# Attention block and selective scan on one core: side steps spaced by their TensorE work, matmuls in smaller pieces

## The chip, the cores and the metric

The kernel runs on one core of a Trainium2 chip. The metric is device time in microseconds: the median over repeated executions. The engines are TensorE (PE in the profile), VectorE (DVE), ScalarE (ACT), GpSimd (POOL) and SyncE (SP), which here issues every DMA. Each engine works off its own instructions in order; between engines, semaphores make one wait for the other.

## The reference

Sixteen images x of 256 channels by 32 x 32 positions go through two layers, each behind a group norm and with a residual (the norms have 16 groups and no weights). In short:

```
# layer 0, per image: tokens n = 1024, channels c = 256
tok  = groupnorm(x).T + pos_embedding
q, k, v = split(layernorm(tok) @ w_qkv)            # 4 heads of 32
out  = softmax(q @ k.T / sqrt(32)) @ v
tok  = out @ w_out + b_out + tok
tok  = gelu(layernorm(tok) @ w_ff1 + b_ff1) @ w_ff2 + b_ff2 + tok
x    = x + tok.T
# layer 1, per image: L = 1024 positions, 512 inner channels, 64 states
xs   = groupnorm(x).T + (rel_h + rel_w)
ctx  = sigmoid(conv1d(xs, gate_w, width 3) + gate_b)
u, z = split(xs @ in_proj_w.T)
u    = silu(depthwise_conv(u, width 4) + conv_b)
dt, Bm, Cm = split(u @ x_proj_w.T, [16, 80])
delta = softplus(dt @ dt_proj_w.T + dt_proj_b);  A = -exp(A_log)
for each position t:                               # for 512 channels d, 64 states n
    h[d, n] = exp(delta[d] * A[d, n]) * h[d, n] + delta[d] * u[d] * Bm[n]
    y[d]    = sum over n of h[d, n] * Cm[n]
x    = x + ((y + u * D) * silu(z)) @ out_proj_w.T * ctx
```

## The kernel before

The scan is the backbone. For one image the recurrence has 512 x 64 = 32768 rows of 1024 positions. The kernel puts two channels with their 64 states on the 128 partitions and cuts time in two halves of 512 positions. A *unit* is four channels over one half: two DVE scans of 128 x 512. There are 256 units per image and 4096 in all; the loop `for n, (b, t, k, q, i) in enumerate(units)` writes them out one after the other. Eight units with the same q are a *block*. I call the 256 units of one image a *pass*. What surrounds unit n in program order is:

- `load(n + 6)`: SP issues the DMA that spreads delta times u over the partitions (`dub`, 512 KB, seven buffers).
- `inputs(n + 4)`: POOL multiplies `dub` by B.
- `scan(n, 0)` and `scan(n, 1)`: the two DVE scans, which read the decay `a` from PSUM and `dub`, and write `h`.
- `decay(n + 2)`: two matmuls (L880) spread delta, and two ACT Exps (L883) make the decay in place. The four PSUM buffers `a` come free as the scans of unit n have read them.
- A piece of *side work*, see below.
- A piece of `outputs`: the products of the states with C for the block before (L927), with a copy to SBUF (L935), a second set of matmuls that turn the result (L939), another copy (L947) and the stores.

The side work is everything else: while image b is being scanned, the rest of image b - 1 (the multiplication with silu(z), the output projection, the gate and the store: `gate_and_store`) and all that comes before the scan for image b + 1 (`first_norm`, `attention_layer`, `scan_inputs`). These are Python generators, and each `yield` ends a step and gives a number, the share of the step just written out. Before the change the loop keeps an account: each unit adds `rate` (the sum of all shares divided by 247 units, 1.11 for most images), and steps are written out as long as the account is above zero:

```
due += rate
while due > 0.0:
    due -= next(side, 1e9)
```

So two steps can fall into one unit, and a long share can be followed by a step in the very next unit. The order of instructions on PE, ACT, DVE and POOL is then fixed as written: a manual dependency chains each instruction to the one before it on its engine. SP's queue keeps its order as well. PSUM is shared: four banks for `a`, one for `yb` (products with C), one for attention's values, and two (`mm`) for all of the side work.

The names that matter below: L387 takes the row maxima of the scores (written by L406), L474 and L482 are the transposed scores and their Exp, L462 the values (together "st/av"); L282 and L306 are the two vector parts of a layer norm, L267 the end of a group norm, L263/L264 and L299/L301 the Ln and Exp between; L506 is the reciprocal of the softmax denominators, which pass through DRAM; L599 multiplies z by its sigmoid (matmul L610, tanh L615); L645 are the convolution taps on u (matmul L631), L685 its silu; L660 the gate's convolution as matmuls; L697 the projection of u to dt, B and C; L716 to L759 the softplus of delta, its split into three bf16 pieces `pc` and the product `du`. `gate_and_store` begins with L790 (add u times D) and L794 (times z), each on 128 x 1024 for four parts d, their operands ys, us, zs fetched by DMA, and ends with the projection L819 and its use in L806/L808. `spread_c` (L909) writes C into the sparse weights `cd` by eight ACT copies, twice per image. `outputs` before the change hands out a block in six pieces:

```
for half in range(2):
    # s = 0, 1: 32 matmuls; yield; s = 2, 3: 32 matmuls
    # copy y2 <- yb; yield
    # 16 turning matmuls; yield (after half 0)
# copy yo <- yb, three more yields, then the stores
```

Of the kernel before, what the change touches and what calls it, by code (L numbers as in the profile page):

```python
# [52 lines left out]
def attention_then_scan_kernel(  # L53
# [176 lines left out]
    def group_norm(src, dst):  # L230
        def sum_of(part, s, k):
            view = part.rearrange("p (h g t) -> p g h t", g=NG, t=2)
            nc.vector.tensor_reduce(s[:, k, :], view, AX.XY, ALU.add)

        def mean_of(s, name):
            m = psum(f"{name}_ps")[:, :NG]
            for k in range(KC):
                nc.tensor.matmul(m, avg, s[:, k, :], start=(k == 0), stop=(k == KC - 1))
            return m

        per = C / (C * L / NG)
        s = small.tile([P, KC, NG], F32, name="gn_s", tag="gn_s")
        sum_of(src[0], s, 0)
        yield 1.2
        sum_of(src[1], s, 1)
        m = mean_of(s, "gn_m")
        yield 1.2
        s = small.tile([P, KC, NG], F32, name="gn_q", tag="gn_s")
        qs = []
        nc.vector.tensor_scalar(m, m, per, None, ALU.mult)  # L250
        for k in range(KC):
            nc.vector.tensor_tensor(grouped(dst[k]), grouped(src[k]), over_group(m), ALU.subtract)
            q = work("gn_sq")
            nc.scalar.activation(q, dst[k], AF.Square)
            qs.append(q)
            yield 1.2
        sum_of(qs[0], s, 0)
        yield 1.2
        sum_of(qs[1], s, 1)
        del qs, q  # L260
        v = mean_of(s, "gn_v")
        yield 1.2
        nc.scalar.activation(v, v, AF.Ln, bias=eps, scale=per)  # L263
        nc.scalar.activation(v, v, AF.Exp, scale=-0.5)  # L264
        yield 1.5
        for k in range(KC):
            nc.vector.tensor_tensor(grouped(dst[k]), grouped(dst[k]), over_group(v), ALU.mult)  # L267
            yield 1.2


    def layer_norm(src, dst, g, b):
        def mean_of(parts, name):
            m = psum(name)
            for k in range(KC):
                nc.tensor.matmul(m, avg, parts[k], start=(k == 0), stop=(k == KC - 1))
            return m

        def centre(h, m):
            qs = []
            for k in range(KC):  # L280
                d = dst[k][:, hs(h)]
                nc.vector.tensor_tensor(d, src[k][:, hs(h)], m, ALU.subtract)  # L282
                q = hwork("ln_sq")
                nc.scalar.activation(q, d, AF.Square)
                qs.append(q)
            return qs

        m = mean_of([t[:, hs(0)] for t in src], "ln_m")
        yield 1
        q0 = centre(0, m)  # L290
        m = mean_of([t[:, hs(1)] for t in src], "ln_m")
        yield 1.2
        q1 = centre(1, m)
        vs = [mean_of(q0, "ln_v")]
        yield 1.2
        vs.append(mean_of(q1, "ln_v"))
        yield 1
        for v in vs:
            nc.scalar.activation(v, v, AF.Ln, bias=eps)  # L299
        for v in vs:  # L300
            nc.scalar.activation(v, v, AF.Exp, scale=-0.5)  # L301
        yield 2
        for h in range(2):
            for k in range(KC):
                d = dst[k][:, hs(h)]
                nc.vector.tensor_tensor(d, d, vs[h], ALU.mult)  # L306
                nc.scalar.activation(d, d, AF.Identity, bias=col(b, k), scale=col(g, k))
            yield 1.2
# [12 lines left out]
    def first_norm(b):  # L321
        xs, tok = [], []
        kept = state[b]["kept"] = dram.tile([C, L], F32, name="kept", tag="kept")
        if "x" in state[b]:
            xs = state[b].pop("x")
        else:
            for go in fetches(xs, x[b]):
                go()
            yield 0.7
        gn = [work("gn") for _ in range(KC)]  # L330
        yield from along(group_norm(xs, gn), fetches(tok, pos))
        for k in range(KC):
            nc.vector.tensor_tensor(tok[k], tok[k], gn[k], ALU.add)
            nc.sync.dma_start(kept[ts(k, P), :], tok[k])
            yield 1.4

    def attention_layer(b):
# [32 lines left out]
        for i, (t, scale) in enumerate(((q4, DH**-0.5), (k4, 1.0))):  # L370
            for hf in range(2):
                ps = psum("qk_ps")
                for k in range(KC):
                    nc.tensor.matmul(
                        ps, wqk_s[:, k, ts(i, P)], xn[k][:, hs(hf)], start=(k == 0), stop=(k == KC - 1)
                    )
                nc.scalar.activation(t[:, hs(hf)], ps, AF.Copy, scale=scale)
                yield 1
# [19 lines left out]
        for c in range(2 * NJ):  # L398
            for hf in range(2):
                maxima()  # L400
                for g in range(2):
                    waiting.append((psum("s_ps"), g, c, hf))
                for h in range(HEADS):
                    g, e = divmod(h, 2)
                    r = ts(h, DH)
                    nc.tensor.matmul(  # L406
                        waiting[g][0][ts(e, 64)], q4[r, ts(c, 64)], k4[r, hs(hf)],
                        start=True, stop=True,
                    )
                if to_space:  # L410
                    to_space.pop(0)()
                yield 1.1
# [6 lines left out]
        yield 1.2  # L419
# [6 lines left out]
        yield 0.7  # L426
# [3 lines left out]
        for g in range(2):  # L430
# [11 lines left out]
            yield 1  # L442
# [10 lines left out]
        for pair in range(HEADS // 2):  # L453
# [3 lines left out]
            for hf in range(2):  # L457
# [11 lines left out]
                for j in range(NJ):  # L469
# [16 lines left out]
                    yield 1.5  # L486
# [11 lines left out]
        yield 0.6  # L498
        nc.sync.dma_start(few, rows[0])
        yield 0.6  # L500
        tok = []
        for go in fetches(tok, kept):
            go()
            yield 0.8
        yield 0.8
        nc.vector.reciprocal(few, few)  # L506
        yield 0.6
        nc.sync.dma_start(rows[1], few)
        yield 0.6
        for h in range(HEADS):  # L510
            nc.sync.dma_start(sums[ts(h, DH)], den[1, h : h + 1].partition_broadcast(DH))
            if h % 2 == 1:
                yield 0.8
        yield 0.8
        yield 0.8
        outs = []
        for hf in range(2):
# [11 lines left out]
            yield 1.5  # L529
# [11 lines left out]
        for hf in range(2):  # L541
            nc.vector.tensor_tensor(xs[hf], xs[hf], tok[hf], ALU.add)
            ps = psum("f1_ps")
            for k in range(KC):
                nc.tensor.matmul(
                    ps, wff1_s[:, k, :], xn[k][:, hs(hf)], start=(k == 0), stop=(k == KC - 1)
                )
            f1.append(ps)
            yield 1.5
# [17 lines left out]
    def scan_inputs(b):  # L567
# [18 lines left out]
        for k in range(KC):  # L586
            nc.vector.tensor_tensor(body[k], body[k], rels[k], ALU.add)
            yield 1.4
# [15 lines left out]
        for d in range(ND):  # L604
            z = work("z")
            for hf in range(2):
# [10 lines left out]
                yield 1  # L617
# [33 lines left out]
        def gate(o, hf, q):  # L651
            if (hf, q) == (0, 0):
                gates["g"] = work("g")
            if q == 0:
# [3 lines left out]
            for i in range(3 * KC):  # L658
                k, t = divmod(i, 3)
                nc.tensor.matmul(  # L660
                    ps[:, ts(q, C)], xp[k][:, ds(first + t, P, 4)], wg_s[:, k, t, :],
                    start=(i == 0), stop=False,
                )
            nc.tensor.matmul(ps[:, ts(q, C)], one_row, gate_b, start=False, stop=True)
# [10 lines left out]
        for d in range(ND):  # L675
            for t in range(2):
# [3 lines left out]
                yield 1.6  # L680
            tap(d, 2)
            nc.scalar.activation(ups[d][:, :L], us[d], AF.Tanh)
            gate(d // 2, d % 2, 0)
            yield 1.6
# [3 lines left out]
            gate(d // 2, d % 2, 1)  # L688
            yield 1.6
# [3 lines left out]
        for hf in range(2):  # L693
            for dst, lo, n in ((dt, 0, RANK), (bc, RANK, 2 * NS)):
                ps = psum("x_ps", n)
                for d in range(ND):
# [3 lines left out]
                    )  # L700
                nc.scalar.copy(dst[:n, hs(hf)], ps)
                yield 1.6
# [31 lines left out]
        for d in range(ND):  # L734
            items = [more(d, *items[0]), begin(d, 1)]
            yield 1
            items[1] = more(d, *items[1])
            rest(*items[0])
            yield 1.4
# [3 lines left out]
            yield 1.7  # L743
# [4 lines left out]
            yield 1.4  # L748
# [4 lines left out]
            yield 1.4  # L753
# [3 lines left out]
            yield 1.4  # L757
# [8 lines left out]
            yield 1.4  # L766
# [4 lines left out]
    GATE = 26.6  # L771

    def gate_and_store(b):
# [8 lines left out]
        for go in come[:4]:  # L782
            go()
            yield 0.7
# [3 lines left out]
        for d in range(ND):  # L788
# [3 lines left out]
            yield 1.3  # L792
# [3 lines left out]
            yield 1.3  # L796
            if d + 1 < ND:
                come.pop(0)()
                yield 0.7
# [13 lines left out]
        for o in range(KC):  # L813
            for hf in range(2):
                ps = psum("m_ps")
                for q in range(2):
# [10 lines left out]
                    yield 1.1  # L827
# [89 lines left out]
    def outputs(b, t, k, q):  # L917
        cd, hbuf = now["cd"], now["h", q % 2]
        out4 = yb[:, 256:].rearrange("p (j a m e) -> p a e j m", a=2, j=2, e=4)
        if t == 0:  # L920
            nc.scalar.copy(now["last"][:, ds(64 * k + 16 * q, 16)], hbuf[:, :, TB - 1])
        for half in range(2):
            for s in range(4):
# [8 lines left out]
                if s == 1:  # L932
                    yield
            y2 = blk.tile([P, 256], F32, name="y2", tag="y2")
            nc.scalar.copy(y2, yb[:, :256])  # L935
            yield
            for e in range(4):
                for s in range(4):
                    nc.tensor.matmul(  # L939
                        out4[32 * s : 32 * s + 16, half, e],  # L940
                        y2[:, 64 * s + e : 64 * s + 64 : 4], turn[:, e],
                        start=True, stop=True,
                    )
            if half == 0:
                yield
# [16 lines left out]
    steps = sum(prepare(0))  # L962
# [9 lines left out]
    side, rate, due = iter(()), 0.0, 0.0  # L972
    for n, (b, t, k, q, i) in enumerate(units):
        at = n % UNITS
        if at == 0:
            parts = [prepare(b + 1)] if b + 1 < B else []
            total = steps * len(parts)
            if b > 0:
# [3 lines left out]
                total += GATE  # L982
            side = chain(*parts)
            rate, due = total / (UNITS - AHEAD - 3), 0.0
# [14 lines left out]
        if at >= (1 if b + 1 < B else 8):  # L999
            due += rate  # L1000
            while due > 0.0:
                due -= next(side, 1e9)
# [85 lines left out]
```

## Time and profile before

| | |
|---|---|
| median of three runs | 13563.83 us (13536.5 to 13569.5) |
| profiled execution | 13520.45 us, its span 13518.5 us |
| DVE busy | 12165.9 us, 90% of the span |
| PE busy (weight loads) | 10686.8 us, 79% (5389.6 us, 40%) |
| POOL busy | 9761.5 us, 72% |
| ACT busy | 7916.0 us, 59% |
| DMA | 209 GB/s in the mean, queue 1 at 60.5% of its 16 engines |
| two scans of a unit | 1199 ns each in the first half of time, 1260 in the second |

The first unit begins 377 us into the span and the last ends at 13472 us, so that nearly the whole time is the unit loop. A busy share over such a loop is a mean over stages that have different limits, and the stages repeat with every image. It is therefore of more use to cut one image's 256 units into their stages, and to ask in each of them what the DVE, the fullest engine, waits for. "Granted clock" is the share of TensorE's full clock that the record shows as granted. A wait is put down to the releaser that came last by the profile; where the engine named had long been done, it was another.

### The profile page before, as it was taken

To read this page: it belongs to the slowest core of one execution; us is meant where nothing else is said; L and a number is where in the kernel's file an instruction comes from. 1 tells how busy PE (TensorE), PEld (TensorE's weight loads), DVE (VectorE), ACT (ScalarE), POOL (GpSimd) and SP (SyncE) were. 2 spreads that over 40 slices of the span, in tenths; PEclk is the share of its full clock that TensorE was granted. 3 is DMA by queue.
4 is the path that set the end of the run, shared out by engine and by line. 5 is a ranking of instruction groups with operands and counts; after the bars stand their busy time and mean duration, and the time that the engine had idled before them with its cause. 6 is when DMAs were issued, how large, how long until landed. Compare 5 with 4: busy or idle time off the path is not lost. (4 is left out here: it accounts for less than half of the span.)

```text
span 13518.5 us, 429250 instructions
## 1 busy us (share of the span) xinstructions
PE 10686.8 (79%) x186800; PEld 5389.6 (40%) x186800; DVE 12165.9 (90%) x11652; ACT 7916.0 (59%) x13941; POOL 9761.5 (72%) x4118
## 2 busy tenths in 40 slices
PE   7787878878787787877878778787787878878767
PEld 3343344433444334443344433434444344433434
DVE  3899999899998999999999898999999999989998
ACT  3666665656655565555656556566465665656654
POOL 0777767777777777767777677776777767777697
PEclk8786877868788686876868778687786877868777
DMA  1566566565665666656666566655666566665666
GB/s 64 202 205 234 197 212 218 203 227 203 208 217 200 228 205 213 212 201 223 208 223 205 198 222 206 235 199 199 220 207 234 193 205 220 206 231 198 209 233 224
DMA packets 1001896, 2820.85 MB, mean 209 GB/s; under 512 B 175810, under 2 KB 319427, under 8 KB 1000004
## 3 DMA queue, kind: packets, MB, share of 16 engines
q1 hardware_dynamic: 1000004, 2793.39, 60.5%
q8 instruction: 1460, 23.92, 0.7%
q14 instruction: 432, 3.54, 0.1%
HBM read 2514.18 MB, written 261.62 MB: 205 GB/s over the span
## 5 line engine op out<-in xcount | busy, mean ns | idle before, releaser
L871 POOL TENSOR_TENSOR dub<-dub,bt 128x1024 f32<-128x1024 f32 x4096 | 9706.4, 2386 | 3702.5 <-DMA dub<-dus 3218.5
L883 ACT ACTIVATE a<-a,acol 128x512 f32<-128x512 f32 x8192 | 5063.6, 659 | 3830.4 <-PE a L880 3800.3
L893 DVE TENSOR_TENSOR_SCAN h<-a,last,dub 128x512 f32<-128x512 f32 x4096 | 4927.0, 1260 | 129.1 <-issue 88.0
L893 DVE TENSOR_TENSOR_SCAN h<-a,dub 128x512 f32<-128x512 f32 x4096 | 4691.0, 1199 | 281.1 <-issue 160.7
L880 PE MATMUL a<-pieces,pick 48*128 48x512 bf16 x8192 | 2983.3, 468 | 2447.9 <-DVE h L893 2371.4
L927 PEld LDWEIGHTS yb<-h,cd 128*32 128x32 f32 x131072 | 2568.5, 136 | 1945.6 <-issue 1700.1
L927 PE MATMUL yb<-h,cd 128*32 128x64 f32 x131072 | 2967.1, 259 | 28.8 <-issue 19.7
L880 PEld LDWEIGHTS <-pick 48*128 48x128 bf16 x8192 | 521.6, 96 | 2607.9 <-issue 2396.6
L406 PE MATMUL s_ps<-k,q 32*64 32x512 f32 x4096 | 890.4, 719 | 59.2 <-DVE mx L387 58.3
L939 PEld LDWEIGHTS yb<-turn,y 128*16 128x16 f32 x32768 | 408.7, 119 | 993.6 <-ACT y L935 493.2
L935 ACT COPY y<-yb 128x256 f32<-128x256 f32 x1024 | 383.3, 374 | 718.3 <-PE yb L927 714.3
L387 DVE TENSOR_REDUCE mx<-s_ps 128x1 f32<-128x512 f32 x1024 | 643.4, 669 | 24.4 <-PE s_ps L406 22.2
L939 PE MATMUL yb<-turn,y 128*16 128x32 f32 x32768 | 538.2, 212 | 103.2 <-ACT y L935 99.4
L474 PE MATMUL st_ps<-sp 33*128 33x512 f32 x2048 | 598.0, 627 | 14.1 <-ACT pt L482 13.9
L462 PE MATMUL av<-pt,vv 128*64 128x512 f32 x2048 | 577.3, 642 | 5.5 <-ACT sums L451 3.3
L482 ACT ACTIVATE pt<-st_ps 128x512 f32<-128x512 f32 x1024 | 556.7, 604 | 40.0 <-PE st_ps L474 38.8
L660 PE MATMUL g_ps<-w,xp 128*128 128x256 f32 x1536 | 447.4, 447 | 0.0
L406 PEld LDWEIGHTS s_ps<-k,q 32*64 32x64 f32 x4096 | 206.8, 148 | 580.1 <-DVE mx L387 540.3
L660 PEld LDWEIGHTS g_ps<-w,xp 128*128 128x128 f32 x1536 | 389.5, 328 | 100.5 <-issue 77.4
L645 DVE SCALAR_TENSOR_TENSOR u<-up,cwh,u 128x1024 f32<-128x1024 f32 x192 | 341.0, 1776 | 32.8 <-ACT u L637 32.5
L819 PE MATMUL m_ps<-w,xs 128*128 128x256 f32 x1024 | 310.4, 451 | 12.3 <-DVE xs L794 12.3
L819 PEld LDWEIGHTS m_ps<-w,xs 128*128 128x128 f32 x1024 | 258.6, 328 | 89.5 <-issue 60.5
(135 smaller groups left out, 7147.0 us busy)
## 6 DMA issues: line engine op xcount, KB each, us to landing
dub<-dus SPq DMA_DIRECT2D x4096, 512.0 KB
dps<-pc SPq DMA_DIRECT2D x384, 128.0 KB
pieces<-dps SPq DMA_DIRECT2D x1024, 48.0 KB
xs<-in_x_dram SPq DMA_DIRECT2D x64, 512.0 KB
xs<-kept SPq DMA_DIRECT2D x64, 512.0 KB
zs<-z SPq DMA_DIRECT2D x64, 512.0 KB
ud<-u SPq DMA_DIRECT2D x64, 512.0 KB
dus<-du SPq DMA_DIRECT2D x64, 512.0 KB
```

Of the source, the lines that this page charges most:

```text
L387: nc.vector.tensor_reduce(mx[:, g, c, hf : hf + 1], s, AX.X, ALU.max)
L406: nc.tensor.matmul(waiting[g][0][ts(e, 64)], q4[r, ts(c, 64)], k4[r, hs(hf)], start=True, stop=True,)
L462: nc.tensor.matmul(av[ts(e, 2 * DH)], vv[j // (NJ // 2)][:, j % (NJ // 2), 2 * pair + e, :], pts[e], start=(j == 0), stop=(j == NJ - 1),)
L474: nc.tensor.matmul(s, ka[r, ts(j, P)], qa[r, hs(hf)], start=True, stop=True)
L660: nc.tensor.matmul(ps[:, ts(q, C)], xp[k][:, ds(first + t, P, 4)], wg_s[:, k, t, :], start=(i == 0), stop=False,)
L819: nc.tensor.matmul(ps[:, ts(q, C)], us[d][:, ds(first, P, 4)], wo_s[:, d, :], start=(d == 0), stop=(d == ND - 1),)
L871: nc.gpsimd.tensor_tensor(v, v, bt.unsqueeze(1).to_broadcast([P, 2, TB]), ALU.mult)
L880: nc.tensor.matmul(a, w, pieces[r], start=True, stop=True)
L883: nc.scalar.activation(a, a, AF.Exp, scale=acol[:, at : at + 1])
L893: nc.vector.tensor_tensor_scan(now["h", q % 2][:, 2 * i + e, :], decays[n][e], loaded[n][:, e, :], first, ALU.mult, ALU.add,)
L927: nc.tensor.matmul(yb[ts(g, 32), ts(s, 64)], cd[:, at // 16, ts(c, 32)], hbuf[:, :, at : at + 4], start=(c == 0), stop=(c == 3),)
L939: nc.tensor.matmul(out4[32 * s : 32 * s + 16, half, e], y2[:, 64 * s + e : 64 * s + 64 : 4], turn[:, e], start=True, stop=True,)
```

## The change

The account is replaced. The shares are re-estimated, step by step, and the loop now counts down the gap to the next step. A share under 1 stands for itself, so that such steps may share a unit; any other share becomes a gap of at least one unit, so that a step with a share of 1 or more is always followed by a new unit. The rate is solved for by bisection, so that the gaps of a batch fill the room of 247 units.

```diff
-    steps = sum(prepare(0))
+    steps = list(prepare(0))
+
+    def gap(share, rate):
+        return share if share < 1 else max(1.0, share / rate)
+
+    def rate_for(shares, room):
+        lo, hi = 0.01, 10.0
+        for _ in range(40):
+            mid = (lo + hi) / 2
+            lo, hi = (mid, hi) if sum(gap(w, mid) for w in shares) > room else (lo, mid)
+        return hi
...
-            rate, due = total / (UNITS - AHEAD - 3), 0.0
+            rate, due = rate_for(total, UNITS - AHEAD - 3), 0.0
...
-            due += rate
-            while due > 0.0:
-                due -= next(side, 1e9)
+            due -= 1.0
+            while due <= 0.0:
+                due += gap(next(side, 1e9), rate)
```

The shares that change most: st/av (L474, L462, L482) 1.5 to 1.75; q and k 1 to 1.5; v 1 to 2.2; z 1 to 1.3; the output projection L819 1.1 to 1.3; layer norm's first steps 1 to 1.5; purely vector steps from 1.2 or 1.4 to 0.6 (L267, L333, L587, L790, L794); plain DMA steps from 0.7 or 0.8 to 0.4 or 0.5, but the steps around the denominators from 0.6 to 1; group norm's 1.2 to 1; softplus 1.4 to 1.1.

x's projection, the gate and the products with C are cut finer:

```diff
         for hf in range(2):
             for dst, lo, n in ((dt, 0, RANK), (bc, RANK, 2 * NS)):
                 ps = psum("x_ps", n)
                 for d in range(ND):
                     nc.tensor.matmul(...)
+                    if d == 1:
+                        yield 1.5
                 nc.scalar.copy(dst[:n, hs(hf)], ps)
-                yield 1.6
+                yield 1.5
...
-            gate(d // 2, d % 2, 0)
-            yield 1.6
+            gate(d // 2, d % 2, 0, 0)
+            yield 1
+            gate(d // 2, d % 2, 0, 1)
+            yield 1.5
             nc.vector.scalar_tensor_tensor(us[d], ups[d][:, :L], 1.0, us[d], ALU.add, ALU.mult)
...
-            gate(d // 2, d % 2, 1)
-            yield 1.6
+            gate(d // 2, d % 2, 1, 0)
+            yield 1
+            gate(d // 2, d % 2, 1, 1)
+            yield 1.5
...
+        def turned(half, y2):
+            for e in range(4):
+                for s in range(4):
+                    nc.tensor.matmul(out4[...], y2[...], turn[:, e], start=True, stop=True)
+
+        y2 = None
         for half in range(2):
             for s in range(4):
                 # 16 products with C
-                if s == 1:
+                if s == 3:
+                    y2 = blk.tile([P, 256], F32, name="y2", tag="y2")
+                    nc.scalar.copy(y2, yb[:, :256])
+                if s == 0 and half == 1:
+                    turned(0, y2)
+                if (half, s) != (0, 0):
                     yield
-            y2 = blk.tile([P, 256], F32, name="y2", tag="y2")
-            nc.scalar.copy(y2, yb[:, :256])
-            yield
-            # 16 turning matmuls
-            if half == 0:
-                yield
+        turned(1, y2)
```

A gate step's last argument is the half of the 256 channels that it sums over. A block's products now come as 32, 16, 16, 16, 16, 16, 16 matmuls and at last the second turn, one piece in each of the block's eight units; the first turn goes with the fourth piece. The stores of a block follow two units later than before. Line numbers after L660 shift: L790 becomes L797, L794 L801, L893 L900, L880 L887, L883 L890, L927 L944, L939 L932, L697 L702.

## The prediction

> **What bounds the kernel now.** I read the page's busy times first, then the busy times by stage of one pass (a pass is one batch's 256 units; this is the fifth), then the DVE's waits in it, then the timeline where TensorE is fast and slow.
>
> ```profile
> span 13518.5 us, 429250 instructions
> PE 10686.8 (79%) x186800; PEld 5389.6 (40%) x186800; DVE 12165.9 (90%) x11652; ACT 7916.0 (59%) x13941; POOL 9761.5 (72%) x4118
> ...
> 3674.60:4509.40 834.80, 667.73 (x11674) 335.28 (x11674) 757.53 (x728) 494.20 (x871) 610.46 (x257) 0.77 0.62 211
> 3715.60:3767.00 51.40, 32.63 (x660) 17.16 (x662) 50.29 (x41) 21.11 (x39) 35.63 (x15) 0.53 0.85 303
> 3839.30:3946.50 107.20, 97.49 (x1597) 36.55 (x1597) 106.54 (x124) 44.70 (x82) 72.72 (x32) 0.86 0.52 171
> 3962.70:4083.00 120.30, 111.54 (x2136) 50.04 (x2140) 105.39 (x93) 101.35 (x191) 105.00 (x45) 0.94 0.63 220
> 4330.40:4366.70 36.30, 35.09 (x529) 18.28 (x527) 26.94 (x24) 19.45 (x35) 23.55 (x10) 0.92 0.57 197
> 4366.70:4478.80 112.10, 78.22 (x1388) 38.86 (x1388) 104.23 (x111) 81.54 (x136) 73.53 (x32) 0.53 0.61 205
> ```
>
> After each time range come its length, then busy time of PE, weight loads, DVE, ACT and POOL, the granted clock, DMA share and GB/s. Over the whole pass the DVE is busy 757.5 of 834.8 us: 77 us idle, and nothing else can be saved, since the change takes no DVE work away. The last five rows are the gate's vector part, the score maxima, the attention values (st/av), x's projection and the softplus. In st/av and in x's projection TensorE is the full engine (111.5 of 120.3, 35.1 of 36.3); in the others the DVE is.
>
> ```profile
> DVE h L893 <- issue: 16.7, 21, 1.8
> DVE h L893 <- POOL dub L871: 12.7, 8, 3.7
> DVE d_ps L729 <- ACT d_ps L725: 7.5, 5, 4.1
> DVE z L599 <- ACT z_t L615: 6.5, 4, 2.5
> DVE xn L306 <- ACT ln_v L301: 6.4, 2, 4.0
> DVE m_ps L806 <- PE m_ps L819: 5.6, 4, 3.5
> DVE gn L267 <- ACT gn_v_ps L264: 3.7, 1, 3.7
> DVE xs L790 <- DMA xs<-ud: 1.1, 1, 1.1
> ```
>
> These waits of the same pass (total us, times, longest) are of two kinds. The scans L893 wait 29.4 us; POOL is put down as the releaser, but it had mostly run well ahead, and the units hit are those with most TensorE work. There the decay matmuls queue behind a side step, and with them ACT's Exp, the scan's other input. The rest are side steps whose own producer ran one unit, or no unit, before them.
>
> ```profile
> 4388.76 1.93 PE L927 MATMUL yb<-h,cd 128*32 128x64 f32 x64
> 4334.12 1.10 PE L927 MATMUL yb<-h,cd 128*32 128x64 f32 x64
> 4340.23 0.39 PE L880 MATMUL a<-pieces,pick 48*128 48x512 bf16 x2
> 4346.02 3.70 PE L697 MATMUL x_ps<-u,w 128*128 128x512 f32 x8
> ```
>
> A half block of products with C takes 1.10 us where TensorE is full and 1.93 in the softplus stage; two decays take 0.39 where it is full. x's four projections take 3.7 us each, in one unit, where the DVE's two scans are over in 2.37.
>
> **The change part by part.** Cutting the trace at each unit's first scan, idle time averaged over the 14 middle passes is 73.7 us per pass. I put the order of both programs' instructions beside it. Shares now sum to 271.3 in 230 steps; the solved rate is 1.180, so a step of 1.75 takes 1.48 units, 1.3 takes 1.10, 1 takes exactly 1. Work per batch is unchanged; only its place moves.
>
> x's projection, 7.7 us idle now: each 3.7 us step is split in two of 1.85. TensorE per unit: 0.39 decays + 1.85 + 0.55 (a quarter block of C) = 2.8 against 2.37, with two empty units among ten. Adding each unit's excess and letting the first 0.8 to 1.2 us pass free (units 88 to 91 show it: TensorE 2.1 us over the scans, 1.2 us of idling) gives 2.6 to 1.8, and 8.9 to 8.4 for the order before, measured 7.7. I take 1.8: gain 5.9.
>
> st/av, 12.4 idle: a step is 1.8 us, decays 0.39, C on average 0.67 (eight quarter pieces of 0.55 and two turns of 0.47 in eight units). Before, in 44 units: 57.6 + 44 x 1.06 = 104 against 99 us of scans. After, in 51 units: 112 against 115, so it fits, by 3%. The same running sum gives 6.7 to 2.6 after and 10.4 to 7.5 before, measured 12.4; I take 5: gain 7.4. The seven units come from the spacing of vector work elsewhere.
>
> v (two steps in one unit, now two apart): 2.6 to 0.6. q and k: 3.7 to 2.7, since it still starts on a slow clock. z: the pair of steps in one unit cost 2.5, the cold first one 2.6; L599 now has a rel addition before it: 6.2 to 3.0. Softplus: the 4.0 us at d=1, where begin and more stood in one unit, goes; the three others keep one unit and their 0.5 to 1.7: 8.6 to 5.2. Layer norm's Ln and Exp with two table loads: ACT needs 5 to 6 us, L306 came one unit later once (4.0) and two later once (2.4); now two both times: 6.4 to 4.9. Group norm: L267 moves one unit away, but in the first one Ln/Exp now shares its unit with spread_c's eight ACT copies of 0.395 us, which hold the next Exps: 6.9 to 4.0. The denominators: write and read get a unit each, but spread_c's 3.2 us is no longer covered by that wait: 3.2 to 2.3. The projection after the gate: 6.0 to 4.6, ten units for nine. Means (L282), f1/f2, first tap: same distance, 7.3 to 6.9. Maxima 0.9 to 1.0.
>
> What gets worse is the gate's vector part. L790 and L794 go from 1.3 units each to 0.6, so 13 loads of 512 KB fall into 8 units. SP is in order, and each side load stands behind a dub load that waits for the scan before. Before, us took about 7.4 us from unit 14's start to its use after unit 16's scan (0.66 idle); now it has two units, 4.5 us, and zs follows in the same unit. 10.5 MB with the dub loads at the 303 GB/s of that stage is 35 us against some 32 of DVE work. I take 1.8 to 5.5, between 1.8 (hidden) and 9 (at 250 GB/s). If dub is late too, POOL's lead (12 us there) pays first. The ys write of a block comes two units later, out at unit 10 of the next pass; ys of the last block is fetched after that.
>
> Smaller C pieces: no matmul added. PE, in order, puts 0.55 instead of 1.10 ahead of the next decays. The last reading of a scan buffer moves from the fifth unit of a block to the seventh, two units before its rewriting; it costs nothing while TensorE is less than a unit behind. That scan, queued with all DVE work after it, would otherwise wait: bounded by 0 and the debt's 1 us, 32 times a pass where TensorE is full. Gate halves: 3.18 + 0.69 per step becomes 1.6 and 2.3, in units that hold a tap or silu of 1.25 to 1.9 on the DVE or are followed by an empty one, so nothing; without that cover a 2.3 us half and 0.94 beside it exceed a bare unit by 0.9, eight times a pass. The stores that move with their steps (kept, zs, ud, dus, dps) wait on SP for their DVE or ACT step as now (zs 230 us over the run), the dub loads behind them; POOL being 12 to 15 us ahead of the scans in those stages covers it, and nothing is counted.
>
> [...] The rows: the clock is 0.53 in the softplus stage, where TensorE is never idle 3 us, and 0.94 in st/av. [...] By the rows, it is how full TensorE is that decides, and cold starts stay. I go by the rows.
>
> **Sum.** After: 1.8+5+0.6+2.7+3.0+5.2+4.9+4.0+2.3+4.6+6.9+1.0+5.5 = 47.5, from 73.7: 26.2 per pass, 14 x 26.2 = 367. The first pass (57 idle, no gate part) about 20; the last, gate part only, loses 3. Gain 384 us against the profiled execution's 13520.45 (span 13518.5 and 2 around it), which lies 0.3% under the median 13563.83. Prediction: 13180. Prologue (377 us) and end are as before. Not counted: DVE operations stretched while POOL works (L790 2166 ns beside 1223 for L542, the same size); over taps, gate and norms an estimated 280 us, which may move by a quarter either way, 70 us.
>
> **Rivals.** (1) TensorE goes cold and the maxima become its stage: slower. For it: some units there show L406 at 2.57 against 1.67, after two thin ones, and all units will now be equally thin. A cold unit is 1.16 + 2.57 + 0.97 = 4.7 against the DVE's 3.42, 1.28 lost; in all 32 units of 14 passes 573 us, less the 384: 13753. It decides from 0.86 us per unit on. Against: the backlog fills TensorE and the clock came back within two units each time (0.86 over the stage). 9%: 6 slower, 3 with the gain just eaten up. (2) The gate part is bound by DMA at the page's mean 209 GB/s: 50 us for 32, 12 more than I count per pass, gain 216: 13350. Against: 303 GB/s there already, at 0.85. 10%. (3) The spacing doesn't relieve st/av: ACT's 2.4 us (two Exps, two pt) also fills the unit and 10 us stays, x keeps 4: gain 280: 13285. For: ACT 101 of 120 there. 16%. (4) Nearly all waits shorter, stretching too: half as much again, 13000. 10%. The forecast itself, 13080 to 13280: 55%.
>
> **Numbers.** Range 13000 to 13380, taking in (2) to (4) with the 70 us. A measurement of this kernel tells 0.3% (about 40 us) from no change. Faster by more: 0.91; within: 0.03; slower: 0.06.
>
> **What would show it.** DVE busy share of a middle pass 0.94; x's stage without 1.6 us waits, d=1's L729 wait gone, st/av waits near 5 us, L797 waiting longer for xs<-ud than the 40 us in all of L790. Wrong if the maxima stage lasts over 3.6 us per unit, if the gate part exceeds 45 us, or if st/av keeps 10 us.

## The result, and the profile after

The changed kernel takes 13367.91 us in the median (13355.66 to 13391.62), the kernel before, on the same chip, 13562.74; the ratio is 0.9862, 95% interval 0.9843 to 0.9881. The kernel is faster by 195 us, inside the range, but the forecast was 13180, a gain of 384 us: half of it did not come. The page of the profile after, then the same stages of the fifth pass as were shown of before (the whole pass, gate's vector part, score maxima, attention values, x's projection, softplus; columns as there):

```profile
span 13353.9 us, 429795 instructions
PE 10875.5 (81%) x186800; PEld 5369.3 (40%) x186800; DVE 12191.0 (91%) x11652; ACT 7901.2 (59%) x13941; POOL 9781.8 (73%) x4118
...
3659.40:4485.40 826.00, 683.26 (x11674) 337.97 (x11674) 760.91 (x727) 493.04 (x871) 613.88 (x258) 0.77 0.64 213
3700.90:3732.10 31.20, 15.04 (x301) 7.97 (x301) 24.67 (x22) 9.40 (x17) 17.07 (x8) 0.50 0.94 340
3806.40:3916.60 110.20, 96.11 (x1667) 34.66 (x1666) 109.88 (x130) 46.17 (x84) 77.71 (x34) 1.00 0.55 177
3930.60:4070.10 139.50, 131.79 (x2506) 59.83 (x2497) 121.14 (x108) 110.96 (x211) 121.83 (x53) 0.91 0.66 219
4319.30:4356.60 37.30, 35.70 (x588) 18.49 (x588) 29.09 (x25) 19.32 (x35) 26.68 (x12) 0.90 0.65 205
4356.60:4459.60 103.00, 73.84 (x1281) 35.86 (x1282) 98.99 (x107) 80.31 (x134) 68.72 (x30) 0.54 0.64 213
```

The pass is 9 us shorter, and the DVE has as much to do as before. The maxima and the softplus now run with 0.3 and 4.0 us between length and DVE work. The attention values do not: 18 us of 139.5 are idle, with the clock at 0.91. In the mean over the 14 middle passes the DVE idles 59.0 us (73.7 before, 47.5 forecast). The waits of the pass (total, times, longest) show what is new:

```profile
DVE h L900 <- PE yb L944: 7.1, 7, 2.4
DVE xs L797 <- DMA xs<-ud: 6.5, 3, 5.4
...
DVE d_ps L736 <- ACT d_ps L732: 2.3, 4, 0.8
```

The first line stood nowhere before: a scan waits for the products with C. The second was 1.1 us, the last 7.5. (A block's 128 products with C count as 256 records, two for each: a quarter, 16 products, is x32.) Here is the end of unit 87 in the timeline (start, duration, engine, instruction; idle time before it in brackets), first the DVE, then PE:

```profile
3944.42 6.93 DVE L900 TENSOR_TENSOR_SCAN h<-a,dub 128x512 f32<-128x512 f32 x6
3952.62 5.68 DVE L900 TENSOR_TENSOR_SCAN h<-a,dub 128x512 f32<-128x512 f32 x5 [1.27 <-PE yb L944]
...
3949.78 1.02 PE L474 MATMUL st_ps<-sp 33*128 33x512 f32 x4
...
3951.74 0.65 PE L944 MATMUL yb<-h,cd 128*32 128x64 f32 x32
...
3953.90 0.37 PE L887 MATMUL a<-pieces,pick 48*128 48x512 bf16 x1 [0.55 <-DVE h L900]
3955.01 0.58 PE L887 MATMUL a<-pieces,pick 48*128 48x512 bf16 x1 [0.74 <-DVE h L900]
3955.03 2.28 PE L474 MATMUL st_ps<-sp 33*128 33x512 f32 x4
```

Unit 88 opens a block and overwrites the states of the block before last. Their last quarter of products, L944, ends at 3952.39, and the scan follows at 3952.62, after 1.27 us of waiting. Then it goes on: the decays wait for the scans to free their banks, TensorE is empty for 0.55 and 0.74 us, and the next scores take 2.28 us where those before took 1.02; the granted clock is 0.50 from 3955.0 to 3959.5. One short wait is followed by a slow unit.

### The profile page after: what moved, and what is told of

It is laid out like the page before. It is cut to its first block, busy times and chain, and to the rows that moved or that the text cites. A ratio compares the mean times of both kernels' runs of the same rounds, so it can differ in the third digit from the quotient of the medians.

```text
span 13353.9 us, 429795 instructions
## 1 busy us (share of the span) xinstructions
PE 10875.5 (81%) x186800; PEld 5369.3 (40%) x186800; DVE 12191.0 (91%) x11652; ACT 7901.2 (59%) x13941; POOL 9781.8 (73%) x4118
## 5 line engine op out<-in xcount | busy, mean ns | idle before, releaser
L890 ACT ACTIVATE a<-a,acol 128x512 f32<-128x512 f32 x8192 | 5058.9, 659 | 4092.5 <-PE a L887 4083.8
L900 DVE TENSOR_TENSOR_SCAN h<-a,last,dub 128x512 f32<-128x512 f32 x4096 | 4934.6, 1262 | 127.9 <-issue 43.2
L900 DVE TENSOR_TENSOR_SCAN h<-a,dub 128x512 f32<-128x512 f32 x4096 | 4687.0, 1203 | 325.8 <-issue 168.0
L887 PE MATMUL a<-pieces,pick 48*128 48x512 bf16 x8192 | 2998.2, 458 | 1969.8 <-DVE h L900 1901.3
L944 PEld LDWEIGHTS yb<-h,cd 128*32 128x32 f32 x131072 | 2568.9, 132 | 3160.4 <-issue 2345.6
L944 PE MATMUL yb<-h,cd 128*32 128x64 f32 x131072 | 3249.6, 257 | 130.4 <-ACT yo L958 91.8
L887 PEld LDWEIGHTS <-pick 48*128 48x128 bf16 x8192 | 502.7, 95 | 1426.5 <-issue 1150.2
L406 PE MATMUL s_ps<-k,q 32*64 32x512 f32 x4096 | 831.7, 615 | 94.3 <-DVE mx L387 94.3
L932 PEld LDWEIGHTS yb<-turn,y 128*16 128x16 f32 x32768 | 458.0, 121 | 509.4 <-ACT y L951 250.2
L474 PE MATMUL st_ps<-sp 33*128 33x512 f32 x2048 | 628.5, 642 | 8.4 <-ACT pt L482 8.4
L462 PE MATMUL av<-pt,vv 128*64 128x512 f32 x2048 | 614.6, 680 | 6.1 <-ACT sums L451 3.3
L932 PE MATMUL yb<-turn,y 128*16 128x32 f32 x32768 | 555.8, 216 | 67.5 <-ACT y L951 67.5
L482 ACT ACTIVATE pt<-st_ps 128x512 f32<-128x512 f32 x1024 | 559.6, 608 | 51.6 <-PE st_ps L474 49.9
L659 PE MATMUL g_ps<-w,xp 128*128 128x256 f32 x1536 | 499.3, 468 | 0.0
L645 DVE SCALAR_TENSOR_TENSOR u<-up,cwh,u 128x1024 f32<-128x1024 f32 x192 | 381.6, 1988 | 23.6 <-ACT u L637 23.3
L474 PEld LDWEIGHTS st_ps<-sp 33*128 33x128 f32 x2048 | 232.3, 198 | 189.8 <-issue 92.4
```

The lines of the kernel that those rows point to most:

```text
L406: nc.tensor.matmul(waiting[g][0][ts(e, 64)], q4[r, ts(c, 64)], k4[r, hs(hf)], start=True, stop=True,)
L462: nc.tensor.matmul(av[ts(e, 2 * DH)], vv[j // (NJ // 2)][:, j % (NJ // 2), 2 * pair + e, :], pts[e], start=(j == 0), stop=(j == NJ - 1),)
L474: nc.tensor.matmul(s, ka[r, ts(j, P)], qa[r, hs(hf)], start=True, stop=True)
L482: nc.scalar.activation(pt, s, AF.Exp)
L659: nc.tensor.matmul(ps[:, ts(q, C)], xp[k][:, ds(first + t, P, 4)], wg_s[:, k, t, :], start=(k == 0 and t == 0), stop=False,)
L887: nc.tensor.matmul(a, w, pieces[r], start=True, stop=True)
```

## Experiments

All were timed beside the kernel before on their chip (13548.63 us for the first four, 13561.09 for the next three, 13565.29 for the last); what is compared is the ratios. One per cent is 136 us.

**The old pieces in the new schedule.** `outputs` as it was before the change, six pieces, last reading in the block's fifth unit:

```diff
-                if (half, s) != (0, 0):
+                if s == 1:
                     yield
...
-        turned(1, y2)
+            # copy y2; yield; the 16 turning matmuls; yield after half 0
```

> The changed kernel with the products with C in their old six pieces; spacing, gate and x's projection as changed. Theory W (the finer pieces move the last reading of a scan buffer to the block's seventh unit, and the first scan of the next block waits for it): the idle before the first scan of a block, 1.2 us each at units 88, 104 and 112 and some 8 us per pass in all, goes, and with it TensorE's idling and slow clock after it; idle per pass falls from 59 to about 46, time to about 13190 us. Theory R (the quarter pieces cost TensorE 0.65 instead of 0.55 us, 20 us more per pass): the same direction and about the same size, 13200, since both are undone here. Theory N (the pieces are no cause; the attention values are simply too dense for the new spacing): 13350 to 13400, and their stage keeps 16 to 18 us of idle.

13348.85 us, ratio 0.9852 (0.9837 to 0.9867); idle 56.4 us per pass. The size that I expected is missed by far: this is hardly better than the change. Cut by unit, the two traces show a gain and a loss that nearly cancel. The idle time before the first scan of a block falls from 9.4 us per pass in the change to 0.5, so the late reading is gone; all other idle time rises by some 6 us, and the pieces are all that differs. In the attention values 16.8 us stay of 17.9, as other waits grow there (3.2 us in unit 82 for 2.2, 2.7 in unit 122 for 1.8); in the stage of the output projection and the second layer norm the idle time is 9.4 us for 7.2.

**The new pieces alone**, in the kernel before, with its account and shares:

```diff
-                if s == 1:
+                if (half, s) != (0, 0):
                     yield
...
+        turned(1, y2)
```

> The kernel before with only the products with C in the new eight pieces. W: waits of the first scan of a block on the products appear wherever TensorE is full (q and k, values, x's projection), 6 to 10 us per pass; 13650 to 13720, slower than before. R: 3 to 4 us more idle in the values' stage, 13610. N: no difference, 13560, or a little faster from the shorter pieces.

13647.11 us, ratio 1.0074 (1.0061 to 1.0087); idle 81.5 us for 73.7. By themselves they make the kernel slower, as the wait theory (W) expected: the idle time before the first scan of a block rises from 3.6 to 15.2 us per pass, and a wait for the products with C, absent before, is there with 80.6 us over the run.

**The new pieces, read earlier.** The last two quarters are done together in a block's sixth unit, the last turn in its seventh; the stores stay where they were:

```diff
-                if (half, s) != (0, 0):
+                if (half, s) not in ((0, 0), (1, 2)):
                     yield
...
-        for _ in range(3):
+        for _ in range(4):
             yield
```

> The changed kernel with one piece of the products moved: the last two quarters of a block in the sixth unit together, the last turn in the seventh; seven pieces, five of them still single quarters, the stores where they are. The last reading of the scan buffer is one unit earlier, which gives it some 2.3 us more. W: the waits before the first scan of a block fall to nearly nothing and the values' stage from 18 to about 9 us of idle; 13190 to 13230. R: six sevenths of the extra TensorE time stay, so 13340 to 13360. N: 13370.

13223.56 us, ratio 0.9761 (0.9747 to 0.9774), where 13190 to 13230 was expected. No `PE yb` stands among the waits of the scans any more; idle time falls from 59.0 to 51.8 us, of it 5.8 in the attention values and 2.1 in x's projection. By unit, the idle time before the first scan of a block falls from 9.4 to 1.8 us per pass, and all other hardly changes: the fall is in the place that the wait theory names. The last reading a unit earlier is worth 137 us. It fits the first run: with the earlier reading the finer pieces are better than the old ones by 0.9% (0.9761 for 0.9852); with the late one that is just used up.

**The gate's vector part at its old spacing**, 1.3 per operation and 0.7 per load:

```diff
-    GATE = [0.4] * 4 + ([0.6, 0.6, 0.4] * ND)[:-1] + [1.3] * 8 + [1]
+    GATE = [0.7] * 4 + ([1.3, 1.3, 0.7] * ND)[:-1] + [1.3] * 8 + [1]
```

> The changed kernel with the old shares in the gate's vector part (1.3, 1.3, 0.7 instead of 0.6, 0.6, 0.4; the four loads ahead of it 0.7), the rest as changed; the solved rate rises to keep the batch in its room. If the close packing of the 13 loads costs what the trace shows (6.5 us before one L797): its 7.5 us of idle per pass fall to about 2, the other steps stand closer and give back 1 to 3; 13300 to 13350. If the room that this packing made is worth more than its wait: the values and x's projection lose 5 us or more and the time is 13370 to 13420.

13467.06 us, ratio 0.9937 (0.992 to 0.9953). In the mean the first L797 of a pass still waits 5.8 us (6.5 in the change), so the dense packing is not its cause. And the run is slower by 0.75%: the units that the packing sets free are worth some 100 us elsewhere (idle in the softplus with the unit before it 7.4 us for 4.7, in the taps and the gate of u 5.5 for 2.6, in the second group norm 3.0 for 0.4). SP's queue shows the cause of the wait in the change (issues of the fifth pass; the first column is when, the second for how long SP was at it), and then the DVE:

```profile
3695.44 3.70 SPq L334 DMA_DIRECT2D kept<-xs  x2
...
3701.55 0.59 SPq L790 DMA_DIRECT2D w<-in_w_o_dram  x1
3702.19 1.37 SPq L314 DMA_DIRECT2D xs<-ud  x1
...
3708.67 1.28 DVE L797 SCALAR_TENSOR_TENSOR xs<-xs,vec 128x1024 f32<-128x1024 f32 x1 [5.42 <-DMA xs<-ud]
```

The load of u is issued at 3702.19 and used at 3708.67, and it stands behind the stores of the tokens, which hold SP until the DVE has added them (L333).

**The first gate loads ahead of those stores**, on top of the early reading:

```diff
         nc.scalar.activation(v, v, AF.Exp, scale=-0.5)   # group norm's step before the last
+        if early:
+            early()                                       # fetch ud, ys, zs of part 0
         yield 1.6
...
-        come.insert(1, bring[0])
+        if "early" in st:
+            ...
+            come = [bring[0]] + come[3:]                  # w_o after them
```

> The kernel with the last reading by unit 5, and the first three loads of the gate's vector part (u, scan output, gate of block 0) issued two units earlier, ahead of the stores of the tokens, which wait on SP for the DVE's additions; the projection's weights come after them. Theory L (late issue): the first L797 waits 6.7 us per pass because us is issued behind those stores and the weights, about 7 us before it can be used. Issued two steps ahead it is there in time: the wait falls under 1.5 us, idle time per pass from 51.8 to 46 to 47, and the run from 13223 to 13140 to 13165. Rival B (bandwidth): in these units SP's loads fill the DMA engines, so an earlier start only moves the wait to the next loads: idle 50 to 52, time 13200 to 13240. Rival S: the earlier loads push the dub loads back and the scans wait instead: slower than 13240.

13197.87 us, ratio 0.9736 (0.9722 to 0.975). The waits came out as theory L had them: idle 45.4 us for 51.8, the gate's part 1.9 for 7.8. The time did not: 34 us for the 59 to 84 expected, and that is little beside the intervals, which touch (0.9747 to 0.9774 for the early reading alone). The two rows of the gate, of the early reading alone and then with the early loads (busy, mean ns | idle before it):

```profile
L797 DVE SCALAR_TENSOR_TENSOR xs<-xs,vec 128x1024 f32<-128x1024 f32 x64 | 107.1, 1674 | 116.2 <-DMA xs<-ud 116.0
L801 DVE TENSOR_TENSOR xs<-xs 128x1024 f32<-128x1024 f32 x64 | 88.4, 1382 | 10.6 <-DMA xs<-zs 9.3
```

```profile
L810 DVE TENSOR_TENSOR xs<-xs 128x1024 f32<-128x1024 f32 x64 | 136.7, 2137 | 5.9 <-DMA xs<-zs 4.7
L805 DVE SCALAR_TENSOR_TENSOR xs<-xs,vec 128x1024 f32<-128x1024 f32 x64 | 113.7, 1776 | 39.3 <-DMA xs<-ud 39.3
```

77 us of waiting are gone, and the two operations last 55 us longer: an L810 takes 2137 ns for 1382. The timeline of the kernel with the early loads says why:

```profile
4494.48 2.79 DVE L810 TENSOR_TENSOR xs<-xs 128x1024 f32<-128x1024 f32 x1
...
4493.84 2.35 POOL L896 TENSOR_TENSOR dub<-dub,bt 128x1024 f32<-128x1024 f32 x1 [2.92 <-DMA dub<-dus]
```

POOL's operation ends at 4496.19, the L810 at 4497.27, 1.08 us later; an L810 that meets no POOL operation takes 1.22 in all. It reads as held until POOL is done, not as slowed throughout. POOL for its part waits for its loads in this stage (the 2.92 us in the bracket), so that it starts when the DVE is in the middle of its work. With the early reading alone 28 of the 64 operations started while POOL worked, with 0.50 us of it left in the mean; with the early loads it is 44, with 1.47. That the earlier loads themselves push POOL's loads back, in the sense of rival B, is not shown. The last section has the count over all of them.

**Thin units filled.** What is left in the attention values are three waits of 2.6 to 2.8 us, and each follows two or three units with little TensorE work. Around the wait in unit 82, in the kernel with the early reading (TensorE, then the DVE, then two stretches of time with the granted clock third from the end):

```profile
3883.30 0.43 PE L887 MATMUL a<-pieces,pick 48*128 48x512 bf16 x1 [0.69 <-DVE h L900]
3883.52 2.32 PE L474 MATMUL st_ps<-sp 33*128 33x512 f32 x4
...
3887.67 1.94 PE L944 MATMUL yb<-h,cd 128*32 128x64 f32 x64
...
3890.96 5.68 DVE L900 TENSOR_TENSOR_SCAN h<-a,dub 128x512 f32<-128x512 f32 x5 [3.26 <-issue]
...
3879.00:3883.00 4.00, 3.15 (x77) 1.49 (x66) 4.00 (x4) 3.42 (x8) 3.56 (x2) 1.00 0.74 218
3883.00:3890.00 7.00, 6.70 (x75) 3.02 (x74) 4.70 (x5) 3.14 (x7) 6.94 (x4) 0.53 0.74 230
```

From 3879 to 3883 TensorE was busy 3.15 of 4 us, its gaps 0.22, 0.24 and, the longest, the 0.69 us of the first line. Then the clock is 0.53 for seven us: the scores take 2.32 for 1.02, half a C group (x64) 1.94 for 1.10, and the scan waits 3.26 us. To see whether it is the clock or simply the amount of work, I added work, on top of the early reading:

```diff
+    WARM = {78: 3, 79: 2, 105: 3, 106: 2, 118: 3, 119: 3}     # unit of the pass: repeats
...
-            nc.tensor.matmul(a, w, pieces[r], start=True, stop=True)
+            for _ in range(1 + more):
+                nc.tensor.matmul(a, w, pieces[r], start=True, stop=True)
```

> The kernel with the last reading by unit 5, and in six units of a pass (78, 79, 105, 106, 118, 119), those around the start and the pair ends of the attention values, each decay matmul is done 2 or 3 times more into the same bank (the result is the same): about 0.8 to 1.2 us more of TensorE work in each, 6 us per pass, none of it useful. Theory C (clock): three units thin in TensorE work bring the half clock in the next full one (L474 2.3 for 1.02, L462 1.97 for 1.08, L944 1.94 for 1.10), and that alone is the wait of 2.6 to 2.8 us before the scans of units 82, 109 and 122, 8.2 of the stage's 12.1 us of idle time. With the thin units filled the clock stays: the stage's idle falls to 4 to 6, the run to 13100 to 13140. Rival F (fullness): the stage simply has more TensorE work than the scans cover, and the waits are where the debt comes due: 6 us more of work make 3 to 6 us more of idle per pass, 13260 to 13310. Between them, no change: the filling was too little or in the wrong place.

13182.35 us, ratio 0.972 (0.9705 to 0.9736); the stage idles 7.5 us for 12.1. More work for the engine that is full in this stage made it idle less, which F excludes. The repeats came to some 3 us per pass (all decay matmuls 2972.7 us over the run for 2924.9), half of what was meant. In time it is 56 us of the 84 to 124 that C expected: waits of 1.1 to 1.3 us remain in units 121 and 109, and what is behind these I did not take apart. The same place as above, the scores and two stretches:

```profile
3880.01 1.50 PE L474 MATMUL st_ps<-sp 33*128 33x512 f32 x4
...
3878.00:3882.00 4.00, 3.26 (x14) 1.00 (x11) 4.00 (x5) 4.00 (x9) 4.00 (x2) 1.00 0.64 203
3882.00:3888.00 6.00, 6.00 (x150) 3.12 (x146) 5.51 (x5) 4.63 (x10) 5.28 (x4) 1.00 0.71 236
```

The granted clock stays at 1.00, and the scores take 1.50 us for 2.32, the half C group after them 1.10 for 1.94. Over the attention values of the 14 middle passes the clock is 0.99 in the mean, for 0.93 with the early reading alone.

So with fuller units the clock stayed up (0.99 for 0.93); how full, and over what time, isn't shown. From 3878 to 3882 the filled kernel is nearly as thin (3.26 of 4 us) and stays at 1.00, and in the kernel with the early reading TensorE is busy 2.36 of 4 us from 3868 to 3872 without a fall of the clock before 3883.

**Thin units joined**, the other way to the same end: the last values of a (pair, half) and their evacuation go into the step of the next first scores, instead of steps of their own. The early reading stays.

```diff
+                    if j == 0 and tail:
+                        tail[0](NJ - 1)
+                        evacuate(*tail[1], 0)
...
-                values(NJ - 1)
-                evacuate(pair, hf, 0)
-                yield 1
+                tail = values, (pair, hf)
```

> The kernel with the last reading by unit 5, and the last values and the evacuation of a (pair, half) done in the same step as the first scores of the next: no step of the attention values is left thin but the very first and the very last; no work is added, six side steps per batch fall away, and all others are spaced 1 to 2% wider. Theory C (clock): two of the three half-clock spells (units 107 and 120) go, 5.4 us per pass: 13140 to 13170. Rival F (fullness): joined steps are fuller (ACT has two Exps and four copies in one unit, 3.7 us) and the waits stay or grow: 13220 to 13260.

13383.07 us, ratio 0.9867 (0.9852 to 0.9882): slower than the early reading alone by 1.1%, worse than either theory had it. ACT in a joined step of the fifth pass, and the scan that waits for it:

```profile
3982.88 0.58 ACT L450 COPY ao<-av 32x512 f32<-32x512 f32 x1 [0.61 <-PE av L463]
...
3984.07 1.08 ACT L486 ACTIVATE pt<-st_ps 128x512 f32<-128x512 f32 x2
...
3985.77 0.58 ACT L451 COPY sums<-av 32x512 f32<-32x512 f32 x1
3986.38 1.24 ACT L895 ACTIVATE a<-a,acol 128x512 f32<-128x512 f32 x2
...
3987.13 3.45 DVE L905 TENSOR_TENSOR_SCAN h<-a,dub 128x512 f32<-128x512 f32 x3 [2.97 <-issue]
```

Four copies of 0.58 and two Exps stand before the decays' Exps L895, and the scan waits 2.97 us; 2.6 to 3.0 us three times a pass. TensorE empties meanwhile (gaps of 0.58 and 0.66 us), and the next L475 takes 2.39 us, for 1.40 in the step before; the clock is 1.00 up to 3986 and 0.86 in the mean from there to 3991. Here the wait came first and the slow clock after it. The rest of the loss came with the shift of the steps that follow (waits for the denominators' two transfers of 2.8 and 3.0 us for 0.6 and 0.4); I did not take it apart.

**All three that helped together** (early reading, early loads, filled units):

> All three together: the last reading by unit 5, the first gate loads ahead of the token stores, and the thin units of the attention values filled with repeated decay matmuls. Theory of separate causes: the gains stand in different stages (gate units 12 to 20; attention values 79 to 132) and add: ratio to the kernel before about 0.9761 - 0.0025 - 0.0041 = 0.9695, that is 13140 to 13160, idle 41 per pass. Rival, one shared limit (what one stage gives is taken back by DVE operations held by POOL or by the scans' inputs elsewhere): no better than the filled one alone, 13175 to 13200.

13142.5 us, ratio 0.9688 (0.9675 to 0.9701), 0.9695 expected from adding: the gains are separate, and the early loads, whose gain alone was hardly beyond the intervals, show it here too (0.9688 with them, 0.972 without). Idle is 42.0 us per pass. It is 3.1% faster than the kernel before and 1.8% faster than the change.

## Why the prediction had the direction right and the size wrong

The direction was right, and so was the mechanism in most stages; the size failed, and so did the attention values by the prediction's own sign (it was to be wrong if they keep 10 us; they kept 17.9). The profiled execution's span fell by 164.6 us, not 384 (that of before lay 0.3% under its median). Of the difference, 161 us is idle time of the middle passes (14 times 11.5), 15 the first pass, which gained 5 instead of 20, 3 the last, and the rest is 28 us of longer DVE operations in the units and an 11 us longer prologue (377 to 407 us in the traces of all these kernels).

| idle us per pass | forecast | measured | with early reading | all three |
|---|---|---|---|---|
| all | 47.5 | 59.0 | 51.8 | 42.0 |
| attention values (units 79 to 131) | 5 | 17.9 | 12.1 | 8.6 |
| x's projection | 1.8 | 4.3 | 2.2 | 2.0 |
| gate's vector part | 5.5 | 7.5 | 7.8 | 2.3 |
| everything else | 35.2 | 29.3 | 29.7 | 29.1 |

*The step that failed first* is the sentence that the last reading of a scan buffer in the seventh unit "costs nothing while TensorE is less than a unit behind", bounded by 1 us and taken as 0. After units 87, 103, 111, 183 and 207 the first scan of a block waits 0.7 to 1.8 us in the mean, over all blocks 9.4 us per pass (3.6 before the change), and the earlier reading gives back 137 of the 189 us that were missing. The end chosen was the wrong one: in the two stages where TensorE is the full engine, the forecast's own running sums let it fall back until the DVE waits, so being behind is the rule there and the upper end belonged in the sum. Nor was the price the wait alone, since the unit after it ran at half clock (0.50 after unit 87, above).

*The second* is the sum for the attention values. It summed, at full clock, 1.8 us of TensorE work per step and 1.06 per unit, and found room of 3%. Three terms are off. A step takes more than 1.8: the scores last 1.02 us and the values 1.08, and from start to start it is 0.96 and 1.01, which the timeline of before has too. A quarter piece of C takes 0.65 us, not half of 1.10 (from start to start 0.59 for half of 1.03; the whole group L944 rose from 2967.1 to 3249.6 us, and with the old pieces in the new schedule it is 2926.7). In the filled kernel, near full clock, TensorE is busy 124 us in the 53 units of the stage, some 3 of it repeats, where the forecast's terms make 114 and the scans take 119 (2.25 each, as in the forecast); so there was no room. And the clock was not counted: in the fifth pass it is 0.95 with the early reading, a mean of full speed and of half-clock spells after thin units, and 1.00 once these are filled. Filling these took 4.6 us of idle out, about two thirds of what stood between 12.1 and the forecast's 5. Rival (3) named the symptoms (10 us kept, and 4 in x's projection, where 4.3 were measured), with ACT as the cause; the filled kernel gives ACT nothing less to do and yet idles less, so ACT is not what held it there.

*The gate's part*, 5.5, was 7.5, near enough, and rival (2), whose 13350 lies close to the result by chance, was not what happened: the part lasts 31.2 us where it was to exceed 45, and its wait is one late issue at its start. The forecast named the stores of the tokens on SP only for the loads of `dub` behind them and counted nothing; they hold the first load of u. That load's wait was 6.5 of the 7.5 us; bought off, it came back in large part (55 of 77 us over the run) as time that POOL holds the DVE.

*Right*: v (0.7 for 0.6), q and k (2.2 for 2.7), the end of the wait at d = 1 of the softplus, and the maxima, which rival (1) made slower: 0.3 us idle in 34 units, clock 1.00. x's projection comes to its forecast only with the early reading (2.2 for 1.8). Somewhat better than forecast: group norms 1.9 for 4.0, z 2.1 for 3.0, denominators 1.0 for 2.3.

*The rows weighed*: I read from the rows of before that how full TensorE is decides its clock. In the fifth pass after the change the softplus stage stays at 0.54, with TensorE busy 72% of it and never idle longer than 2.4 us, and the gate's part is at 0.50, with TensorE busy 48% of it and, with u late, idle 7.5 us at a stretch; the first use of the projection behind it still waits 3.5 us. So far the rows held. But I didn't carry their reading into the stage that was fast: the attention values stood at 0.94 before, and the sum took full clock; now no gap there is longer than 0.9 us, and the clock is 0.91. Nor does a stage's mean fullness decide alone: the maxima, 87% busy, run at 1.00, the values, 94% busy, at 0.91.

## What to carry to other kernels

Cutting an engine's work into finer pieces moves its last reading of a buffer; before you count that as free (one unit was worth 137 us here), ask how far behind that engine is where it is full, and put the last reading a unit earlier rather than later. Where a stage's mean clock lies between half and full, as TensorE's did here (0.91 in the attention values, where every record of the clock, before and after the change, is 0.50 or 1.00), it is not a constant: look for the thin units, and either fill them (worth 56 us here) or leave them where nobody waits. And when a wait is taken away, look at the durations of the operations behind it (an L810 took 2137 ns for 1382), not only at the idle time.

## Not expected of the hardware

- **POOL held the DVE entirely.** In the kernel with the early loads, 44 of 64 L810 (two SBUF inputs) started while POOL's multiplication ran, with 1.47 us of it left in the mean; they took 2.55 us, and the duration is that time left plus 1.09 us (slope 1.0, correlation 1.00). The 18 that met no POOL operation took 1.224, and the two during which POOL began 1.225. The scans, which read their decay from PSUM, took 1.23 us with POOL running and 1.24 without; what sets them apart was not shown. I had the stretch in the prediction as a fluctuation of 70 us; for the L810 it was the order of starts.
- **The half clock came without a long gap.** Four us with TensorE 79% busy and no gap over 0.7 us were followed by seven at 0.53. That didn't always happen: four us that were 59% busy, with gaps up to 0.74, were not followed by it.
- **A split group of matmuls was dearer than its share**: 32 records of L944 in 0.65 us, 64 in 1.10; from start to start 0.59 and 1.03.
